# A LoRA layer folded into a mixture of low-rank experts: W dealt by strided rows, B turned on VectorE, G sent through DRAM

## The chip, the core and the metric

The kernel runs on one core of one Trainium2 chip, in one launch. The metric is the device time of that core in microseconds. All data are float32. The engines are TensorE (PE in the profile, with PEld for its weight loads), VectorE (DVE), ScalarE (ACT), GpSimd (POOL) and SyncE (SP); SyncE only issues DMAs here. All DMAs of the core share 16 DMA engines.

## The reference

```python
# x: 8 x 512 x 2048; W: 2048 x 2048; b: 2048
# lora_As: 32 x 2048 x 16; lora_Bs: 32 x 16 x 2048; one slot for each batch row
# route_w: 8 x 2048; A: 8 x 16 x 2048; Bw: 8 x 2048 x 16
A_b = lora_As[slot]; B_b = lora_Bs[slot]
y = einsum('bti,oi->bto', x, W) + b + 2.0 * einsum('btr,bro->bto', einsum('bti,bir->btr', x, A_b), B_b)
logits = einsum('bsd,ed->bse', y, route_w)
top_v, top_i = top_k(logits, 1)
weight = one_hot(top_i, 8) * top_v
h = einsum('bsd,erd->bser', y, A)
out = x + einsum('bser,eor->bso', weight[..., None] * h, Bw)
```

y itself is never needed, only its products with 136 columns: the 8 x 16 rows of A and the 8 rows of route_w, which the kernel calls proj (2048 x 136).

## The kernel before

**What it computes.** In a first stage the kernel forms C = W^T proj (2048 x 136), the bias row c0 = b proj, and G = 2 B proj, where B holds the 16 rows of each of the eight batch rows' slots, 128 rows in all. The matrix of batch row b is M_b = C + A_b G_b. The second stage multiplies each of the 32 token tiles of x (128 tokens x 2048) by its M_b (`heads`, ph), adds c0 and routes on VectorE (`route`), turns the routed 128 columns (`turn_heads`, pw), multiplies by ffn_b (`delta`, po) and adds the result to x (`add_delta`).

**The first stage.** W comes in 16 tiles of 128 rows (`load_w`, four buffers, SyncE's queue). For each, `chunk_w` copies the two halves of the tile's columns into an order of its own, the first on ScalarE and the second on VectorE (wv, two buffers each), and then the next free W buffer is loaded. `fold_w` multiplies the 16 chunks of a tile by that tile's rows of proj (pj), into six banks of PSUM (pc) that sum over the 16 tiles. A float32 matmul counts as two passes, so a W tile is 32 passes.

**Around it.** The order of every engine's work is written by hand: each engine takes its instructions in the order of the program, under a manual schedule, and a loop over oc (the W tiles) places everything else between the W products:
- `load_adapters_b` (after tile 4) works out the row numbers of B on VectorE and GpSimd gathers them from memory (raw, first half); `load_adapters_a` (after tile 7) does the same for A. The bias is loaded on GpSimd's queue.
- `turn_adapters` (tiles 8 to 10) transposes B in 16 TensorE transposes into pbT, and ScalarE copies them to ad_bT.
- `fold_bias` (tiles 9 and 10) sums bias times proj on VectorE, 16 instructions, into bp.
- `project_bias` and `project_adapters` (after tile 11) are the matmuls pb and pg; VectorE takes G to g_sb.
- `spread_g` (after tile 12 and within tile 13) brings the 32 rows of G of each pair of batch rows to all four quadrants of 32 partitions, by four matmuls with `eyes`, four stacked identities, into pq; VectorE multiplies each by a half mask into g4.
- `first_products` are the products A_0 G_0 (pa) from quadrants of 32 rows; they stand after tile 13, within 14 and after 14. After tile 15 VectorE adds them to C (m) and ScalarE keeps C (c).
- `spread_a` and `shuffle` copy A and x into quadrants, on GpSimd and ScalarE; `turn_x` transposes x on VectorE in blocks of 32 x 32 into xT.

Lines of before that the text names: L132 warm matmuls, L101 W loads, L95 proj loads, L274 W copies, L285 W products (pc), L316 and L317 B transposes and their copies, L307 and L309 bias products, L323 pb, L330 pg, L333 g_sb, L339 pq, L348 g4, L361 pa, L452 ph.

**DMA queues.** Plain loads and stores are issued by SyncE (q1 in the profile) and ScalarE (q10), gathers by GpSimd (q0). Eight semaphores take turns over the DMAs of SyncE and ScalarE, so a DMA waits for the earlier one on its semaphore. SyncE issues in order; after W come ffn_b (fb) and x_1 and x_2, in two tiles of 1 MB each.

Of the kernel before, what the change touches and what calls it, by code (L numbers as in the profile page):

```python
# [9 lines left out]
F32 = mybir.dt.float32  # L10
# [8 lines left out]
def kernel(  # L19
# [27 lines left out]

    nc = tc.nc  # L50
    P = 128
    Q = 32
# [21 lines left out]
    qpool = ctx.enter_context(tc.tile_pool(name="qpool", bufs=2))  # L74
    tpool = ctx.enter_context(tc.tile_pool(name="tpool", bufs=3))
    small = ctx.enter_context(tc.tile_pool(name="small", bufs=2))
    wctx = ctx.enter_context(ExitStack())
    wpool = wctx.enter_context(tc.tile_pool(name="wpool", bufs=1))
    ps_s = ctx.enter_context(tc.tile_pool(name="ps_s", bufs=2, space=bass.MemoryType.PSUM))
# [9 lines left out]

    it_i = const.tile([P, B], I32, name="it_i")  # L90
    pj = wpool.tile([P, NO, NP], F32, name="pj")
    proj_v = proj.rearrange("(c p) e -> p c e", p=P)

    def load_pj(c0, c1, eng=nc.sync):
        eng.dma_start(out=pj[:, c0:c1, :], in_=proj_v[:, c0:c1, :])  # L95
# [2 lines left out]

    def load_w(oc):
        wt = wpool.tile([P, D], F32, tag="w", bufs=4, name=f"w_{oc}")  # L100
        nc.sync.dma_start(out=wt, in_=w[ts(oc, P), :])  # L101
        w_tiles.append(wt)

    load_pj(0, 1, nc.scalar)
    load_w(0)
    load_w(1)
    load_pj(3, 5)
    load_w(2)
    load_pj(5, 8)
    load_w(3)  # L110

    x_tiles = {}
# [12 lines left out]
    make_identity(nc, ident)  # L125

    nc.scalar.copy(warm_a[:, 1:2], warm_a[:, :1])
    load_pj(1, 3, nc.scalar)
    nc.scalar.dma_start(out=it_i, in_=itok.to_broadcast([P, B]))
    pm = ps_s.tile([P, P], F32, tag="s", name="pm")  # L130
    for _ in range(14):
        nc.tensor.matmul(pm, warm, warm, start=True, stop=True)  # L132

    own_i = const.tile([P, B], I32, name="own_i")
# [11 lines left out]
    rank = const.tile([P, E], F32, name="rank")  # L146
    nc.vector.tensor_copy(rank, rank_i)

    raw = qpool.tile([P, 2, D], F32, tag="q", name="raw")
    ad_b = raw[:, 0, :]  # L150
    ad_ar = raw[:, 1, :]
    fb = const.tile([P, D], F32, name="fb")
    bias_o = const.tile([P, NO], F32, name="bias_o")

    brow_f = const.tile([P, 1], F32, name="brow_f")

    def load_adapters_b():

        it_f = const.tile([P, B], F32, name="it_f")
        nc.vector.tensor_scalar(it_f, it_i, float(R), None, ALU.mult)  # L160
        row_f = const.tile([P, B], F32, name="row_f")
        nc.vector.tensor_tensor(row_f, it_f, own, ALU.add)
        nc.vector.tensor_tensor(row_f, row_f, mask, ALU.mult)
        nc.vector.tensor_reduce(brow_f, row_f, AX.X, ALU.add)
        brow_i = const.tile([P, 1], I32, name="brow_i")
        nc.vector.tensor_copy(brow_i, brow_f)  # L166
        nc.gpsimd.indirect_dma_start(  # L167
            out=ad_b,
            out_offset=None,
            in_=cond_b,  # L170
            in_offset=bass.IndirectOffsetOnAxis(ap=brow_i, axis=0),
        )
        nc.gpsimd.dma_start(out=bias_o, in_=bias)

    def load_adapters_a():

# [8 lines left out]


    half = const.tile([P, 2], F32, name="half")

    def fill_constants():
        nc.vector.tensor_reduce(  # L190
            half, mask.rearrange("p (k h) -> p h k", h=2), AX.X, ALU.add
        )

# [8 lines left out]
    def spread_a(q, k, copy):  # L204
# [3 lines left out]
        if q < 2:  # L208
            copy(dst[:, 3:], src[:, ds(JC + 2 * q, 2)])

    ad_bT = tpool.tile([P, NJ, P], F32, tag="t", name="ad_bT")

    g4 = const.tile([P, B, NP], F32, name="g4")
# [4 lines left out]
    def turn(dst, src, h):  # L218
# [2 lines left out]
            dst[:, ts(h, HJ), :].rearrange("p j (g t) -> p g j t", t=Q),  # L221
            src.rearrange("p g (j a) -> p g j a", a=Q)[:, :, ts(h, HJ), :],
        )


    eyes = const.tile([P, NQ, Q], F32, name="eyes")
    nc.vector.tensor_reduce(
        eyes[:, 0, :], ident.rearrange("p (q c) -> p c q", c=Q), AX.X, ALU.add
    )
    nc.vector.tensor_copy(eyes[:, 1:, :], eyes[:, :1, :].to_broadcast([P, NQ - 1, Q]))  # L230

    xq_tiles = {}
    moves = [(g, i) for i in range(NQ) for g in range(NQ)]
# [26 lines left out]
    def chunk_w(oc):  # L260
        copies = (nc.scalar.copy, nc.vector.tensor_copy)
        wv = [
            wpool.tile([P, HJ, P], F32, tag=f"wv{h}", bufs=2, name=f"wv{h}_{oc}")
            for h in range(2)
        ]
        wr = w_tiles[oc].rearrange("p (i j a) -> p j i a", i=NQ, a=Q)
        for h in range(2):
            wv_tiles[oc, h] = wv[h]
            dst = wv[h].rearrange("p j (i a) -> p j i a", a=Q)

            n = HJ // 2 if oc == 0 else HJ
            for k in range(HJ // n):
                copy = copies[1 - k] if oc == 0 else copies[h]
                copy(dst[:, ts(k, n)], wr[:, ds(h * HJ + k * n, n)])  # L274
        if oc + 4 < NO:
            if oc in (0, 1):
                load_pj(8 + 4 * oc, 12 + 4 * oc)
            load_w(oc + 4)

    def fold_w(oc, within=None):  # L280
        for q, (pc, (j0, n)) in enumerate(zip(pcs, groups)):
            for k in range(n):

                h, j = divmod(j0 + k, HJ)
                nc.tensor.matmul(  # L285
                    pc[:, k, :],
                    wv_tiles[oc, h][:, j, :],
                    pj[:, oc, :],
                    start=(oc == 0 and k == 0),
                    stop=(oc == NO - 1),  # L290
                    skip_group_check=True,
                )
            if oc == NO - 1:
                k, jk = divmod(j0, JC)
                c, m = (part[k][:, ds(jk, n), :] for part in (cs, ms[0]))
                nc.vector.tensor_tensor(m, m, pc[:, :n, :], ALU.add)
                nc.scalar.copy(c, pc[:, :n, :])
            if q == 2 and within:
                within()


    bp = wpool.tile([P, NP], F32, name="bp")

    def fold_bias(js):
        for j in js:
            if j == 0:
                nc.vector.tensor_scalar(bp, pj[:, 0, :], bias_o[:, :1], None, ALU.mult)  # L307
            else:
                nc.vector.scalar_tensor_tensor(  # L309
                    bp, pj[:, j, :], bias_o[:, j : j + 1], bp, ALU.mult, ALU.add  # L310
                )

    def turn_adapters(g):
        pt = ps_s.tile([P, 4, P], F32, tag="s", name=f"pbT_{g}")
        for k in range(4):
            nc.tensor.transpose(pt[:, k, :], ad_b[:, ts(4 * g + k, P)], ident)  # L316
        nc.scalar.copy(ad_bT[:, ts(g, 4), :], pt)  # L317

    g_sb = wpool.tile([P, NP], F32, name="g_sb")

    def project_bias():
        pb = ps_s.tile([P, NP], F32, tag="s", name="pb")
# [9 lines left out]
            )  # L332
        nc.vector.tensor_scalar(g_sb, pg, COND_SCALING, None, ALU.mult)  # L333

    def spread_g(ks):

        for k in ks:
            pq = ps_s.tile([P, NP], F32, tag="s", name=f"pq_{k}")
            nc.tensor.matmul(  # L339
                pq,  # L340
                eyes[ts(k, Q)].rearrange("p q c -> p (q c)"),
                g_sb[ts(k, Q), :],
                start=True,
                stop=True,
                tile_position=(k * Q, 0),
            )
            for h in range(2):
                nc.vector.tensor_scalar(  # L348
                    g4[:, 2 * k + h, :], pq, half[:, h : h + 1], None, ALU.mult
                )  # L350


    pieces = [(0, 3 * q, 3, q) for q in range(NQ)] + [(1, 2 * q, 2, q) for q in range(2)]
# [17 lines left out]
        part, j0, nj, _ = pieces[z]  # L371
        return (t[part][:, ds(j0, nj), :] for t in (ms[b % 2], cs))

    def first_products(some, copy=nc.vector.tensor_copy):
        banks = {
            z: ps_s.tile([P, GRP, NP], F32, tag="s", name=f"pa_{z}") for z in some
        }
        adapter_products(0, some, banks)
        for z in some:
            m, _ = place(0, z)  # L380
            copy(m, banks[z][:, : pieces[z][2], :])

    chunk_w(0)
    for oc in range(NO):
        if oc + 1 < NO:
            chunk_w(oc + 1)
        fold_w(
            oc,
            {
                13: lambda: spread_g((2, 3)),  # L390
                14: lambda: first_products((2, 3)),
            }.get(oc),
        )
        if oc == 2:
            fill_constants()
        if oc == 4:
            load_adapters_b()
        if oc == 7:
            load_adapters_a()
        for g in {8: (0,), 9: (1, 2), 10: (3,)}.get(oc, ()):  # L400
            turn_adapters(g)
        if oc in (9, 10):
            fold_bias(range(8 * (oc - 9), 8 * (oc - 8)))
        if oc == 8:
            load_x(0)
            for k in range(NQ):
                for q in range(3):
                    spread_a(q, k, nc.gpsimd.tensor_copy)
            shuffle(0, moves[6:], nc.gpsimd.tensor_copy)
        if oc == 11:  # L410
            for k in range(NQ):
                spread_a(3, k, nc.scalar.copy)
            nc.sync.dma_start(out=fb, in_=ffn_b)
            load_x(1)
            load_x(2)
            project_bias()
            project_adapters()
        if oc in (12, 13, 14):
            shuffle(0, moves[2 * (oc - 12) : 2 * (oc - 11)], nc.scalar.copy)
        if oc == 12:  # L420
            spread_g((0, 1))
        if oc == 13:
            first_products((0, 1))
        if oc == 14:
            first_products((4, 5), nc.scalar.copy)
            for h in range(2):
                turn_x(0, h)
    wctx.close()
# [254 lines left out]
```

## Time and profile before

| | before |
|---|---|
| median of 3 runs | 326.51 us (326.3 to 326.63) |
| profiled execution | 326.17 us, span 324.4 us |
| TensorE busy | 318.7 us (98%), granted clock 1.0 |
| VectorE, ScalarE, GpSimd busy | 230.1, 185.4, 164.9 us |
| DMA | 88.52 MB, mean 273 GB/s |
| first stage ends (first ph) | 76.86 us |

The times come from one profiled execution. The page gives the busy time of each engine, the span in 40 slices (each digit is the busy share in tenths), the DMA queues, and the chain of work that ended last. The timeline lists instructions in order of time: start, length, engine, line, operation, output and inputs, count, and in brackets the idle time before and what ended it. Matmuls overlap, so a row's length reaches past the start of the next one; lengths of steps on TensorE are taken from start to start.

### The profile page before, as it was taken

Reading aid. Unit: us, or ns where it says so; the run is one execution under the profiler, and the core shown is the slowest. Engines: PE = TensorE matmul, PEld = TensorE weight load, DVE = VectorE, ACT = ScalarE, POOL = GpSimd, SP = SyncE. Lnnn points to the kernel's source line nnn. Section 1 sums busy time; section 2 is a strip of 40 time slices with the busy share of each in tenths; the row PEclk is TensorE's granted clock in tenths of the full one; section 3 lists DMA queues with packets and bytes.
Section 4 is the critical chain, followed back from the end, with each engine's and each line's share of the span. In section 5 each row is a group of like instructions: output and inputs, shape, how many; then the busy total and the mean of one; then the engine's idle time right before and its main releaser. Section 6 shows DMA issues by size and latency. Waiting matters only on the chain.

```text
span 324.4 us, 5611 instructions
## 1 busy us (share of the span) xinstructions
PE 318.7 (98%) x2168; PEld 252.6 (78%) x2168; DVE 230.1 (71%) x408; ACT 185.4 (57%) x230; POOL 164.9 (51%) x180
## 2 busy tenths in 40 slices
PE   8999999999999999999999999999999999999994
PEld 8999999999776777777768677767676777766762
DVE  2123183468879788887887888788787887888864
ACT  3223247527958567748764976596567758770000
POOL 1002149998967676257717771946295357710000
PEclk9999999999999999999999999999999999999999
DMA  7999999953933385859395949585876759334437
GB/s 281 365 404 421 420 418 420 421 231 120 401 129 129 131 284 235 301 233 368 153 375 229 361 165 395 184 353 165 355 255 266 270 250 358 162 162 179 174 144 250
DMA packets 15306, 88.52 MB, mean 273 GB/s; under 512 B 1696, under 2 KB 4016, under 8 KB 4912
## 3 DMA queue, kind: packets, MB, share of 16 engines
q1 hardware_dynamic: 14112, 85.45, 67.2%
q0 software_dynamic: 320, 2.11, 1.6%
q10 hardware_dynamic: 848, 0.61, 0.6%
q8 instruction: 17, 0.28, 0.4%
q14 instruction: 9, 0.07, 0.1%
HBM read 54.60 MB, written 33.55 MB: 272 GB/s over the span
## 4 chain that ended last, share of the span: by engine, by line
PE 94%; DMA 4%; SPq 0%; ACT 0%; DVE 0%; issue 0%; DVEq 0%; ACTq 0%
PE ph L452 37%; PE po L546 32%; PE pc L285 16%; PE pa L361 4%; DMA w<-in_w_dram 4%; PE pg L330 1%; PE pw L508 1%; PE pe_o L546 1%; PE pbT L316 1%; PE pe_h L546 1%; ACT wv L274 0%; DVE x L559 0%; PE pq L339 0%; PE pe_s L546 0%; SPq L101 0%; SPq L95 0%
## 5 line engine op out<-in xcount | busy, mean ns | idle before, releaser
L242 POOL COPY xq<-x 32x1024 f32<-32x1024 f32 x121 | 126.7, 1047 | 77.4 <-DMA x<-in_x_dram 26.7
L242 ACT COPY xq<-x 32x1024 f32<-32x1024 f32 x135 | 140.9, 1044 | 12.0 <-DMA x<-in_x_dram 10.0
L452 PEld LDWEIGHTS ph<-m,xT 128*128 128x128 f32 x1024 | 124.7, 190 | 20.6 <-issue 16.1
L452 PE MATMUL ph<-m,xT 128*128 128x136 f32 x1024 | 129.5, 280 | 0.0
L546 PE MATMUL po<-fb,whT 128*128 128x512 f32 x240 | 111.6, 592 | 0.0
L559 DVE TENSOR_TENSOR x<-x,po 128x1024 f32<-128x1024 f32 x60 | 72.9, 1216 | 30.6 <-PE po L546 30.4
L220 DVE STREAM_TRANSPOSE xT<-xq 128x1024 f32<-128x1024 f32 x64 | 78.9, 1236 | 2.4 <-ACT xq L242 2.4
L546 PEld LDWEIGHTS po<-fb,whT 128*128 128x128 f32 x240 | 41.7, 190 | 32.0 <-issue 32.0
L285 PE MATMUL pc<-pj,wv 128*128 128x136 f32 x512 | 61.7, 280 | 0.2 <-ACT wv L274 0.2
L285 PEld LDWEIGHTS pc<-pj,wv 128*128 128x128 f32 x512 | 60.1, 190 | 1.1 <-ACT wv L274 0.4
L513 ACT COPY whT<-pw 128x128 f32<-128x128 f32 x32 | 8.5, 267 | 54.8 <-PE pw L508 54.5
L274 DVE COPY wv<-w 128x1024 f32<-128x1024 f32 (+1 forms) x17 | 12.7, 754 | 30.8 <-PE pc L285 17.8
L274 ACT COPY wv<-w 128x1024 f32<-128x1024 f32 (+1 forms) x17 | 16.9, 998 | 28.5 <-DMA w<-in_w_dram 21.8
L504 POOL TENSOR_TENSOR m<-m,c 128x408 f32<-128x408 f32 (+1 forms) x28 | 24.5, 905 | 1.3 <-ACT m L499 0.8
L499 ACT COPY m<-pa 128x408 f32<-128x408 f32 (+1 forms) x28 | 10.4, 456 | 17.6 <-PE pa L361 17.6
L167 POOL DMA_INDIRECT raw<-in_cond_b_dram,brow_i x1 | 1.4, 1434 | 24.4 <-DVE brow_i L166 24.4
L361 PE MATMUL pa<-g,ad_q 32*128 32x136 f32 x256 | 12.7, 288 | 0.0
L361 PEld LDWEIGHTS pa<-g,ad_q 32*128 32x128 f32 x256 | 10.6, 184 | 1.3
L207 POOL COPY ad_q<-raw 32x384 f32<-32x384 f32 x12 | 6.4, 536 | 9.3 <-DMA raw<-in_cond_a_dram,arow_i 8.9
L508 PEld LDWEIGHTS pw<-ident,wh 128*128 128x128 f32 x32 | 4.5, 141 | 7.4 <-issue 7.2
L463 DVE TENSOR_TENSOR ph<-ph,c0b 128x136 f32<-128x136 f32 x32 | 9.1, 284 | 1.5 <-PE ph L452 1.5
L473 DVE TENSOR_TENSOR wh<-ph,rw 128x128 f32<-128x128 f32 x32 | 9.3, 291 | 1.1
(65 smaller groups left out, 119.7 us busy)
## 6 DMA issues: line engine op xcount, KB each, us to landing
x<-in_x_dram SPq DMA_DIRECT2D x32, 1024.0 KB, 9.3
out_dram<-x SPq DMA_DIRECT2D x30, 1024.0 KB, 4.9
w<-in_w_dram SPq DMA_DIRECT2D x16, 1024.0 KB, 11.4
out_dram<-x SPq DMA_DIRECT2D x6, 256.0 KB, 2.7
fb<-in_ffn_b_dram SPq DMA_DIRECT2D x1, 1024.0 KB, 13.7
pj<-in_proj_dram SPq DMA_DIRECT2D x2, 272.0 KB, 10.8
out_dram<-x ACTq DMA_DIRECT2D x1, 256.0 KB, 2.4
pj<-in_proj_dram SPq DMA_DIRECT2D x1, 204.0 KB, 11.3
```

Source lines behind the costliest of these rows:

```text
L220: nc.vector.transpose(dst[:, ts(h, HJ), :].rearrange("p j (g t) -> p g j t", t=Q), src.rearrange("p g (j a) -> p g j a", a=Q)[:, :, ts(h, ...
L242: copy(xq_tiles[u][ts(i, Q), :, g, :], x_tiles[u][ts(g, Q), :, ts(i, DQ)])
L274: copy(dst[:, ts(k, n)], wr[:, ds(h * HJ + k * n, n)])
L285: nc.tensor.matmul(pc[:, k, :], wv_tiles[oc, h][:, j, :], pj[:, oc, :], start=(oc == 0 and k == 0), stop=(oc == NO - 1), skip_group_check= ...
L361: nc.tensor.matmul(banks[z][:, n, :], ad_q[ts(q, Q), b // 2, 3 * part + n, :], g4[ts(q, Q), b, :], start=True, stop=True, tile_position=(q ...
L452: nc.tensor.matmul(ph_tiles[t][:, :NP], xT_tiles[t][:, j, :], m[j // JC][:, j % JC, :], start=(j == 0), stop=(j == NJ - 1),)
L463: nc.vector.tensor_tensor(ph, ph, c0b, ALU.add)
L473: nc.vector.tensor_tensor(wh.rearrange("p (e r) -> p e r", r=R), ph[:, :ER].rearrange("p (e r) -> p e r", r=R), rw.unsqueeze(2).to_broadca ...
L499: nc.scalar.copy(m, pa)
L504: nc.gpsimd.tensor_tensor(m, m, c, ALU.add)
L546: nc.tensor.matmul(part, whT_tiles[t], fb[:, ds(c, n)], start=True, stop=True)
L559: nc.vector.tensor_tensor(xs, xs, part, ALU.add)
```

## The change

W is dealt by rows 16p + c instead of 128c + p: tile c holds, on partition p, row 16p + c of W, and pj holds the rows of proj in the same order, so that each partition's rows of proj are contiguous in memory. C is a sum over all rows and does not depend on the order; the bias and the columns of B must follow it.
- Tile 0 is loaded in two DMAs, each with half of the columns; proj comes in four loads (columns 0, 1-2, 3-7, 8-15) instead of six. Three warm matmuls are left out.
- The bias is loaded on ScalarE's queue at the start, in the old order. In `fill_constants` VectorE builds two sums of the identity and the product bias_m, one TensorE matmul (pb_o) puts the bias in order, VectorE copies it. `fold_bias` moves to tiles 6 and 7.
- B is turned without TensorE: `spread_b` copies 16 blocks of 32 x 512 into quadrants (bq; 4 on ScalarE, 12 on VectorE, tiles 8 and 9) and `turn_b` transposes them on VectorE, two halves (tiles 10 and 11).
- G goes to the quadrants through memory: after tile 12's copies are issued ScalarE writes g_sb to DRAM (g_dram), reads it back in four DMAs (gq, `spread_g`), and VectorE multiplies by the half mask in two instructions (`halve_g`, after tile 13). The three groups of `first_products` move by half a tile: within 14, after 14, within 15, and all their copies are on ScalarE. After tile 15 the copies of C wait for two groups.
- In the program load_x(2) stands after project_adapters.

On the engines: ScalarE issues the write of G behind its W copy for tile 13, then shuffles two blocks of x, then issues the four reads, then copies W tile 14. VectorE's products `halve_g` stand between its W copies for tiles 14 and 15. By the DMAs' semaphores x_1's second tile is issued when W tile 15 has landed, x_2's first when ffn_b has landed, and its second when the write of G has landed; before, their waits were for W tiles 12 and 13 and x_0.

```diff
-    proj_v = proj.rearrange("(c p) e -> p c e", p=P)
+    proj_v = proj.rearrange("(p c) e -> p c e", p=P)
+    w_v = w.rearrange("(p c) d -> c p d", p=P)
...
-        nc.sync.dma_start(out=wt, in_=w[ts(oc, P), :])
+
+        n = HJ if oc == 0 else NJ
+        for k in range(NJ // n):
+            dst, src = (
+                m.rearrange("p (i c) -> p i c", i=NQ)[:, :, ds(k * n * Q, n * Q)]
+                if oc == 0
+                else m
+                for m in (wt, w_v[oc])
+            )
+            nc.sync.dma_start(out=dst, in_=src)
         w_tiles.append(wt)
...
-    load_pj(3, 5)
+    load_pj(1, 3)
     load_w(2)
-    load_pj(5, 8)
+    load_pj(3, 8)
...
-    load_pj(1, 3, nc.scalar)
     nc.scalar.dma_start(out=it_i, in_=itok.to_broadcast([P, B]))
     pm = ps_s.tile([P, P], F32, tag="s", name="pm")
-    for _ in range(14):
+    for _ in range(11):
...
-    raw = qpool.tile([P, 2, D], F32, tag="q", name="raw")
-    ad_b = raw[:, 0, :]
-    ad_ar = raw[:, 1, :]
+    ad_b = tpool.tile([P, NJ, P], F32, tag="t", name="ad_b").rearrange("p j a -> p (j a)")
+    ad_ar = qpool.tile([P, 2, D], F32, tag="q", name="ad_ar")[:, 0, :]
     fb = const.tile([P, D], F32, name="fb")
+    bias_n = const.tile([P, NO], F32, name="bias_n")
+    nc.scalar.dma_start(out=bias_n, in_=bias)
...
-        nc.gpsimd.dma_start(out=bias_o, in_=bias)
...
     def fill_constants():
         nc.vector.tensor_reduce(
             half, mask.rearrange("p (k h) -> p h k", h=2), AX.X, ALU.add
         )
+
+        nm = P // NO
+        by_c = wpool.tile([P, NO], F32, name="by_c")
+        nc.vector.tensor_reduce(
+            by_c, ident.rearrange("p (m c) -> p c m", c=NO), AX.X, ALU.add
+        )
+        by_m = wpool.tile([P, nm], F32, name="by_m")
+        nc.vector.tensor_reduce(
+            by_m, ident.rearrange("p (m c) -> p m c", c=NO), AX.X, ALU.add
+        )
+        nc.vector.tensor_tensor(
+            bias_m,
+            bias_n.unsqueeze(2).to_broadcast([P, NO, nm]),
+            by_m.unsqueeze(1).to_broadcast([P, NO, nm]),
+            ALU.mult,
+        )
+        pb = ps_s.tile([P, NO], F32, tag="s", name="pb_o")
+        nc.tensor.matmul(
+            pb, bias_m.rearrange("p k m -> p (k m)"), by_c, start=True, stop=True
+        )
+        nc.vector.tensor_copy(bias_o, pb)
...
+    bq = tpool.tile([P, NQ, DQ], F32, tag="t", name="bq")
     ad_bT = tpool.tile([P, NJ, P], F32, tag="t", name="ad_bT")
...
-    eyes = const.tile([P, NQ, Q], F32, name="eyes")
-    nc.vector.tensor_reduce(
-        eyes[:, 0, :], ident.rearrange("p (q c) -> p c q", c=Q), AX.X, ALU.add
-    )
-    nc.vector.tensor_copy(eyes[:, 1:, :], eyes[:, :1, :].to_broadcast([P, NQ - 1, Q]))
...
-            if oc in (0, 1):
-                load_pj(8 + 4 * oc, 12 + 4 * oc)
+            if oc == 0:
+                load_pj(8, 16)
             load_w(oc + 4)
 
     def fold_w(oc, within=None):
+        kept = []
...
                 k, jk = divmod(j0, JC)
                 c, m = (part[k][:, ds(jk, n), :] for part in (cs, ms[0]))
                 nc.vector.tensor_tensor(m, m, pc[:, :n, :], ALU.add)
-                nc.scalar.copy(c, pc[:, :n, :])
+                kept.append((c, pc[:, :n, :]))
             if q == 2 and within:
                 within()
+            if q >= 2:
+                for c, m in kept:
+                    nc.scalar.copy(c, m)
+                kept.clear()
...
-    def turn_adapters(g):
-        pt = ps_s.tile([P, 4, P], F32, tag="s", name=f"pbT_{g}")
-        for k in range(4):
-            nc.tensor.transpose(pt[:, k, :], ad_b[:, ts(4 * g + k, P)], ident)
-        nc.scalar.copy(ad_bT[:, ts(g, 4), :], pt)
+    def spread_b(ms, copy):
+        for g, i in ms:
+            copy(bq[ts(i, Q), g, :], ad_b[ts(g, Q), ts(i, DQ)])
+
+    def turn_b(h):
+        nc.vector.transpose(
+            ad_bT[:, ts(h, HJ), :].rearrange("p c (g t) -> p g c t", t=Q),
+            bq.rearrange("p g (a c) -> p g c a", c=NO)[:, :, ts(h, HJ), :],
+        )
 
     g_sb = wpool.tile([P, NP], F32, name="g_sb")
+    g_dram = dram.tile([P, NP], F32, name="g_dram")
+    gq = wpool.tile([P, NQ, NP], F32, name="gq")
...
-    def spread_g(ks):
-
-        for k in ks:
-            pq = ps_s.tile([P, NP], F32, tag="s", name=f"pq_{k}")
-            nc.tensor.matmul(
-                pq,
-                eyes[ts(k, Q)].rearrange("p q c -> p (q c)"),
-                g_sb[ts(k, Q), :],
-                start=True,
-                stop=True,
-                tile_position=(k * Q, 0),
+    def spread_g():
+
+        for q in range(NQ):
+            nc.scalar.dma_start(
+                out=gq[ts(q, Q)], in_=g_dram.rearrange("(k s) e -> s k e", s=Q)
             )
-            for h in range(2):
-                nc.vector.tensor_scalar(
-                    g4[:, 2 * k + h, :], pq, half[:, h : h + 1], None, ALU.mult
-                )
+
+    def halve_g():
+
+        for h in range(2):
+            nc.vector.tensor_scalar(
+                g4.rearrange("p (k h) e -> p h k e", h=2)[:, h],
+                gq,
+                half[:, h : h + 1],
+                None,
+                ALU.mult,
+            )
...
-            copy(m, banks[z][:, : pieces[z][2], :])
...
+        if oc == 12:
+            nc.scalar.dma_start(out=g_dram, in_=g_sb)
         fold_w(
             oc,
             {
-                13: lambda: spread_g((2, 3)),
-                14: lambda: first_products((2, 3)),
+                14: lambda: first_products((0, 1)),
+                15: lambda: first_products((4, 5)),
             }.get(oc),
...
+        if oc in (6, 7):
+            fold_bias(range(8 * (oc - 6), 8 * (oc - 5)))
         if oc == 7:
             load_adapters_a()
-        for g in {8: (0,), 9: (1, 2), 10: (3,)}.get(oc, ()):
-            turn_adapters(g)
-        if oc in (9, 10):
-            fold_bias(range(8 * (oc - 9), 8 * (oc - 8)))
...
             shuffle(0, moves[6:], nc.gpsimd.tensor_copy)
+        if oc in (8, 9):
+            ms_b = moves[oc % 2 :: 2]
+            spread_b(ms_b[:2], nc.scalar.copy)
+            spread_b(ms_b[2:], nc.vector.tensor_copy)
+        if oc in (10, 11):
+            turn_b(oc - 10)
         if oc == 11:
             for k in range(NQ):
                 spread_a(3, k, nc.scalar.copy)
             nc.sync.dma_start(out=fb, in_=ffn_b)
             load_x(1)
-            load_x(2)
             project_bias()
             project_adapters()
+            load_x(2)
         if oc in (12, 13, 14):
             shuffle(0, moves[2 * (oc - 12) : 2 * (oc - 11)], nc.scalar.copy)
         if oc == 12:
-            spread_g((0, 1))
+            spread_g()
         if oc == 13:
-            first_products((0, 1))
+            halve_g()
         if oc == 14:
-            first_products((4, 5), nc.scalar.copy)
+            first_products((2, 3))
             for h in range(2):
                 turn_x(0, h)
```

More of the change, by code (lines that the diff above doesn't have):

```diff
@@ L76 @@
     small = ctx.enter_context(tc.tile_pool(name="small", bufs=2))
+    dram = ctx.enter_context(tc.tile_pool(name="dram", bufs=1, space=bass.MemoryType.DRAM))
     wctx = ctx.enter_context(ExitStack())
@@ L187 @@
     half = const.tile([P, 2], F32, name="half")
+    bias_m = wpool.tile([P, NO, P // NO], F32, name="bias_m")
     def fill_constants():
@@ L372, in place, with first_products @@
         return (t[part][:, ds(j0, nj), :] for t in (ms[b % 2], cs))
-    def first_products(some, copy=nc.vector.tensor_copy):
+    def first_products(some):
         banks = {
@@ L380, in first_products @@
             m, _ = place(0, z)
-            copy(m, banks[z][:, : pieces[z][2], :])
+            nc.scalar.copy(m, banks[z][:, : pieces[z][2], :])
     chunk_w(0)
```

## The prediction

> **What bounds the kernel now.** I read the page first: engine totals, slices, chain.
>
> ```profile
> PE 318.7 (98%) x2168; PEld 252.6 (78%) x2168; DVE 230.1 (71%) x408; ACT 185.4 (57%) x230; POOL 164.9 (51%) x180
> DMA  7999999953933385859395949585876759334437
> PE 94%; DMA 4%; SPq 0%; ACT 0%; DVE 0%; issue 0%; DVEq 0%; ACTq 0%
> ```
>
> TensorE is busy 98% of the span and is 94% of the chain. A step taken off it shortens the kernel by its own length, and a wait put on it lengthens it. The second line says what else is scarce, but only early: the DMA engines are full through the whole of the first stage.
>
> Next the timeline of TensorE in that stage; the first number is the start, the second the length.
>
> ```profile
> 1.06 6.16 PE L132 MATMUL pm<-warm 128*128 128x128 f32 x28 [1.06 <-DVE warm_a L87]
> 14.87 26.21 PE L285 MATMUL pc<-pj,wv 128*128 128x136 f32 x224 [0.23 <-ACT wv L274]
> 40.92 0.60 PE L316 MATMUL pbT<-ident,raw 128*128 128x128 f32 x4
> 41.36 3.87 PE L285 MATMUL pc<-pj,wv 128*128 128x136 f32 x32
> ...
> 57.73 3.87 PE L285 MATMUL pc<-pj,wv 128*128 128x136 f32 x32
> 61.53 0.50 PE L339 MATMUL pq<-g_sb,eyes 32*128 32x136 f32 x4
> 61.96 2.35 PE L285 MATMUL pc<-pj,wv 128*128 128x136 f32 x18
> 64.25 0.50 PE L339 MATMUL pq<-g_sb,eyes 32*128 32x136 f32 x4
> 64.68 1.89 PE L285 MATMUL pc<-pj,wv 128*128 128x136 f32 x14
> 66.50 0.96 PE L361 MATMUL pa<-g,ad_q 32*128 32x136 f32 x12
> ...
> 76.86 6.65 PE L452 MATMUL ph<-m,xT 128*128 128x136 f32 x56
> ```
>
> Start to start, 32 passes of a W tile take 3.72 us (26.05/224 a pass, 14.87 to 40.92). The only idle time is 0.4 us before 14.87, behind the third W tile. The second stage starts at 76.86 and is TensorE alone to the end, so the question is when that row starts afterwards.
>
> Last the DMA queues, q1 (SyncE's) and q10 (ScalarE's), in stretches: packets, MB, share of the engines. Two for 2.5 to 6 us, then q1 alone for 66 to 67 and for 68 to 69. Below them are two landings from the page.
>
> ```profile
> q1 hardware_dynamic: 168, 1.25, 86.2%
> q10 hardware_dynamic: 164, 0.08, 8.4%
> q1 hardware_dynamic: 60, 0.41, 98.6%
> q1 hardware_dynamic: 48, 0.33, 79.0%
> ```
> ```profile
> pj<-in_proj_dram ACTq DMA_DIRECT2D x1, 136.0 KB, 7.9
> it_i<-in_itok_dram ACTq DMA_DIRECT2D x1, 4.0 KB, 9.6
> ```
>
> From 2.5 to 6 us both queues have work, and each sends as many packets as the other, 168 against 164, though q1's are 8 KB and q10's 544 bytes or less. Such a pair takes 16 x 3.5/164 = 0.34 us on an engine. So a small load on ScalarE's queue moves at the pace of the large packets: 512 little rows (128 and 256 of proj, 128 of itok), issued from 0.74, had landed only at 1.68 + 9.6 = 11.3. And q1 stays full until 68: that is W, then ffn_b and four x tiles.
>
> **Part by part.** *B on VectorE instead of TensorE.* The 16 transposes go: 0.44 (40.92 to 41.36), 0.87 and 0.44, together 1.75 us off the path. The 16 quarter copies (12 VectorE, 4 ScalarE) and two stream transposes lie beside the W products: six copies at 0.4 (the 128x512 copy) and a W copy of 0.7 to 0.8 are 3.2 of a 3.72 us tile, and the last transpose (1.24) ends near 51, before pg needs it at 52.4. Cost nothing; uncovered, 1.2.
>
> *Masked bias.* VectorE gets two reductions (0.37, the eyes row), a product (about 0.3) and a copy after its fourth W copy, which ended at 17.7; the product is ready near 18.8 and TensorE comes by at 18.59. One small matmul plus that wait: between 0.23 (the pb row) and 0.6; I take 0.5. The two blocks of bias products (8 x 0.37 each) move from tiles 9, 10 to 6, 7 and stand ahead of arow_i on VectorE: the A gather leaves at 37.8 instead of 34.7. GpSimd's spreads and shuffles behind it then end at 69.6 instead of 66.6; VectorE turns x_0 by 72.1, which is covered as long as the second stage starts after 73.
>
> *Head.* Three warm matmuls fewer (six passes of 0.21, 1.3 us), W tile 0 in two halves of 1 KB rows, proj in rows of 1 to 4 KB instead of 544 bytes. Tile 0's first half can be used near 5.8, but tiles 1 and 2 decide: they come behind 1024 packets of 1 KB, at 0.05 each (between 544 bytes at 0.035 and the 1.2 KB mean of the last stores at 0.059) 3.2 us per engine where eight of 0.29 took 2.3; fewer little rows give back 0.5 to 1.5. So from 0.6 lost to 1.3 won; I take 0.4 won.
>
> W's rows now lie 128 KiB apart in memory; no transfer of this trace has such a pitch, so a loss there can't be excluded from the rows (second rival). The Trainium skill, "DMA: Bandwidth & Descriptors", section "Latency and other measured facts", has copies falling from 207 GB/s at a pitch of 512 KiB to 103 at 4 MiB, with about 214 as the full rate; no run here shows it, and read downwards it would make 128 KiB cost nothing.
>
> *G.* The four pq matmuls go: 4.23 - 3.72 = 0.51 for the first pair and 4.54 - 3.72 - 0.19 (the switch into pa, which stays) = 0.63 for the second, 1.14 in all. In their place: g_sb, a write to DRAM, four reads, two products on VectorE, and only then pa(0,1), in the middle of tile 14. pg ends at 57.73 - 1.75 + 0.5 - 0.4 = 56.1, g_sb at 56.6. From there TensorE needs 3.72 x 2 + 2.3 us and would reach pa(0,1) at 65.9.
>
> The write has 128 rows of 544 bytes, like the first proj load on the same queue, which was issued at 0.74 and had landed by 6.2, when SyncE's wait for it ended: 5.5 us. The other end is the store on that queue late in the kernel, 2.4. q1 is as full as at the start, so 5.5: landed at 62.1. Only then does ScalarE issue the reads, 4 x 0.4 us. Its W copy for tile 14 stands behind them and ends at 64.8, where TensorE wants it at 63.6; a stall that vanishes in the next one.
>
> The reads are 512 rows, 32 per engine and four semaphore packets. The first moves near 63.4. q1 ran dry about 69.2 before; with some 1.7 us less of small proj rows, 0.8 more for tile 0 and 0.3 for G's write, now near 68.6. That leaves 5.2/0.29 = 18 large packets per engine: 18 pairs of 0.34 take until 69.5, the rest 18 x 0.03 until 70. The last x tile, issued about 51.9, landed 19.8 later at 71.7, some 2 after its queue ran dry; the same lag puts G at 71.8. Ends: 63.6 (a write in 2.4, reads in 1.6 + 3.0, the short store) and 72.6 (62.1 + the 10.5 of the 512 rows at the start).
>
> The page of the skill named above says, in "Queues, rings and completion order", that an engine drains a packet of some 9 to 17 descriptors from one ring before it turns to the next. By that, G's nine per engine would go in one turn and the reads in four, landing near 66. The 168 against 164 say otherwise, and I go by them.
>
> Products of 544 columns lie between 0.35 (136 columns) and 0.8 (the copy of 1024): two at 0.45, so pa(0,1) starts at 72.8 and TensorE has waited 6.9 us. Behind the waiting instruction on VectorE stand its W copy for tile 15 and the turning of x_0, neither late again. From pa(0,1) to the second stage it is 0.89 + 1.82 + 0.90 + 2.28 + 0.66 + 1.75 = 8.3, so 81.1 against 76.86: +4.2.
>
> Then the clock after the pause. The granted clock reads 1.0 even at the start, yet there TensorE, coming from rest, took 0.21 us a pass for 28 passes and 0.116 later: 2.6 us lost. No row shows a pause in mid-kernel, so 0 to 2.6. The start is the nearest row, the pause is shorter: I take 1.8.
>
> Sum against the profiled execution, 326.17 (span 324.4): +4.2 + 1.8 = 332.2. The median of the runs shown lies 0.3 higher; I leave it at 332.2.
>
> **Rivals.** *G in time (faster).* If q1 is dry or yields, all 1.75 + 1.14 + 0.4 - 0.5 = 2.8 us are won: 323.4. It decides at a landing of 64.8 for no stall, and the change breaks even with 67.6 (76.86 - 8.3 - 1.0). For it: x_1's second tile and x_2 now wait for earlier landings before they are issued, so q1's backlog is shorter. Against: w_15, ffn_b and x_1's first tile keep it fed until each next one is issued; I find no gap.
>
> *W's pitch (slower still).* The last W tile landed near 59 and is needed near 69, so W may lose 10 us over 16 tiles of 2.5 us, a quarter of its rate, before TensorE waits at the end; at half rate the last tile comes 40 us late and the kernel takes some 354. A loss of a quarter shows first at tiles 2 to 4, 1 to 2 us each. Nothing in the profile speaks for it.
>
> *G late by a little.* Landing about 67.6: 326.
>
> **How the numbers follow.** Late G 0.72, by itself 328 to 336 (landing 70 to 72.6 with the clock's 0 to 2.6, head and lag loose by 1). G in time 0.16, slightly late 0.04, pitch 0.08. About 0.2%, 0.65 us, is what a measurement can tell from no change. Faster 0.18, same 0.03, slower 0.79. The range reaches down to the faster case, 323.3, and leaves out the pitch and the edges.
>
> **What would show it.** Right: no idle TensorE until tile 14, then 5 to 7 us before the first pa row with VectorE's g product as releaser and that waiting on DMA gq; q10 and q1 with equal packets from 63 to 68; ph from 81 to 83. Wrong: gq landing before 66; W copies waiting on DMA after tile 4; an A spread or x_0's turn as the last to be ready; pbT's cover gone, with pg waiting for ad_bT.

## The result, and the profile after

The changed kernel takes 335.04 us (median of 6 runs, 332.89 to 337.65) against 326.44 before (6 runs): a ratio of 1.0265, 95% interval 1.0222 to 1.0309. It is slower, as forecast, and 2.8 us above the 332.2 of the prediction, inside its range. The profiled execution took 337.65 us (span 335.9). It is the slowest of the six, and its mean granted clock, 0.978, the lowest (0.983 to 0.989 in the others, 1.000 before), so the lines below overstate the median's loss of 8.6 us by some 3.

The page of the changed kernel, the lines shown before (engines, granted clock in tenths, chain):

```profile
PE 322.1 (96%) x2140; PEld 255.6 (76%) x2140; DVE 235.9 (70%) x414; ACT 187.2 (56%) x234; POOL 163.0 (49%) x179
PEclk9999999975999999999999999999999999999999
PE 89%; DMA 7%; DVE 1%; ACTq 0%; ACT 0%; SPq 0%; issue 0%; DVEq 0%
```

DMA has 7% of the chain instead of 4, and two of the forty slices have a clock well below full. The timeline of TensorE in the first stage, then, from the whole timeline, ScalarE's and VectorE's part, and from the chain of waits the two DMAs of G:

```profile
12.20 7.68 PE L313 MATMUL pc<-pj,wv 128*128 128x136 f32 x64 [1.03 <-ACT wv L301]
...
57.23 7.58 PE L313 MATMUL pc<-pj,wv 128*128 128x136 f32 x64
67.52 3.78 PE L313 MATMUL pc<-pj,wv 128*128 128x136 f32 x18 [2.71 <-ACT wv L301]
75.11 1.73 PE L400 MATMUL pa<-g,ad_q 32*128 32x136 f32 x12 [3.81 <-DVE g L383]
76.77 3.54 PE L313 MATMUL pc<-pj,wv 128*128 128x136 f32 x14
...
88.22 3.98 PE L497 MATMUL ph<-m,xT 128*128 128x136 f32 x33
```
```profile
64.39 1.94 ACTq L376 DMA_DIRECT2D gq<-g_dram  x4
66.42 1.04 ACT L301 COPY wv<-w 128x1024 f32<-128x1024 f32 x1 [6.12 <-issue]
74.11 2.04 DVE L383 TENSOR_SCALAR g<-gq,half 128x544 f32<-128x544 f32 x2 [12.19 <-DMA gq<-g_dram]
```
```profile
57.77 6.60 DMA g_dram<-g_sb
65.86 8.12 DMA gq<-g_dram
```

The second stage starts at 88.22 instead of 76.86, 11.4 us later, and the profiled executions differ by 11.5: all of the loss lies ahead of that row. G leaves at 57.77, is in memory at 64.39 and back at 74.0. Meanwhile TensorE has two pauses: the first W product of tile 14 waits for ScalarE's W copy, which stands behind the reads, and pa(0,1) waits for VectorE's product of the reads. The third part of the loss shows in the stretches of time; the last three numbers of a row are the granted clock, the DMA share and GB/s:

```profile
71.30:75.10 3.80, 0.00 (x1) 0.02 (x1) 0.99 (x2) 0.00 (x0) 3.62 (x5) 0.95 0.14 36
75.10:80.20 5.10, 5.09 (x26) 4.64 (x26) 2.73 (x3) 2.99 (x4) 4.93 (x5) 0.50 0.00 0
80.20:83.00 2.80, 2.80 (x18) 2.51 (x18) 2.14 (x2) 0.90 (x2) 2.68 (x4) 0.50 0.00 0
83.00:85.80 2.80, 2.80 (x15) 2.70 (x14) 1.16 (x2) 0.00 (x0) 0.87 (x1) 0.59 0.00 0
85.80:88.20 2.40, 2.40 (x23) 2.23 (x23) 1.16 (x2) 1.60 (x5) 0.00 (x0) 1.00 0.04 7
```

After the pause TensorE works at half the clock, by the 0.59 of the fourth row until about 85.3, and waits for nobody: from pa(0,1) to ph it is 13.1 us instead of 8.3.

### The profile page after: what moved, and what is told of

It is laid out like the page before. It is cut to its first block, busy times and chain, and to the rows that moved or that the text cites. A ratio compares the mean times of both kernels' runs of the same rounds, so it can differ in the third digit from the quotient of the medians.

```text
span 335.9 us, 5566 instructions
## 1 busy us (share of the span) xinstructions
PE 322.1 (96%) x2140; PEld 255.6 (76%) x2140; DVE 235.9 (70%) x414; ACT 187.2 (56%) x234; POOL 163.0 (49%) x179
## 4 chain that ended last, share of the span: by engine, by line
PE 89%; DMA 7%; DVE 1%; ACTq 0%; ACT 0%; SPq 0%; issue 0%; DVEq 0%
PE ph L497 36%; PE po L591 31%; PE pc L313 15%; PE pa L400 4%; DMA w<-in_w_dram 3%; DMA gq<-g_dram 2%; DMA g_dram<-g_sb 2%; PE pg L368 1%; PE pw L553 1%; PE pe_o L591 1%; PE pe_h L591 1%; ACTq L376 0%; ACT wv L301 0%; DVE x L604 0%; SPq L113 0%; DVE g L383 0%
## 5 line engine op out<-in xcount | busy, mean ns | idle before, releaser
L313 PE MATMUL pc<-pj,wv 128*128 128x136 f32 x512 | 66.6, 294 | 4.4 <-ACT wv L301 3.7
L313 PEld LDWEIGHTS pc<-pj,wv 128*128 128x128 f32 x512 | 65.0, 203 | 5.6 <-ACT wv L301 4.1
L400 PE MATMUL pa<-g,ad_q 32*128 32x136 f32 x256 | 14.2, 303 | 3.8 <-DVE g L383 3.8
L400 PEld LDWEIGHTS pa<-g,ad_q 32*128 32x128 f32 x256 | 12.0, 197 | 5.4 <-issue 4.3
L179 POOL DMA_INDIRECT ad_b<-in_cond_b_dram,brow_i x1 | 1.1, 1128 | 24.5 <-DVE brow_i L178 24.5
L240 POOL COPY ad_q<-ad_ar 32x384 f32<-32x384 f32 x12 | 6.0, 499 | 10.9 <-DMA ad_ar<-in_cond_a_dram,arow_i 10.4
L383 DVE TENSOR_SCALAR g<-gq,half 128x544 f32<-128x544 f32 x2 | 2.0, 1062 | 12.2 <-DMA gq<-g_dram 12.2
## 6 DMA issues: line engine op xcount, KB each, us to landing
w<-in_w_dram SPq DMA_DIRECT2D x15, 1024.0 KB, 11.5
```

What stands on the lines that cost most here:

```text
L313: nc.tensor.matmul(pc[:, k, :], wv_tiles[oc, h][:, j, :], pj[:, oc, :], start=(oc == 0 and k == 0), stop=(oc == NO - 1), skip_group_check= ...
L400: nc.tensor.matmul(banks[z][:, n, :], ad_q[ts(q, Q), b // 2, 3 * part + n, :], g4[ts(q, Q), b, :], start=True, stop=True, tile_position=(q ...
```

## The experiments

**G by matmuls, the rest of the change kept.** The old `spread_g` in its old places; the pa products in the new ones.

```diff
-            nc.scalar.dma_start(out=g_dram, in_=g_sb)          # and the four reads, halve_g
+            spread_g((0, 1))                                   # after tile 12; (2, 3) within tile 13
```

> The changed kernel with G brought to the quadrants by the four matmuls of before (tile 12 and within tile 13) instead of through DRAM; W by strided rows, the two halves of tile 0, the masked bias and B on VectorE stay, and so do the new places of the pa products. Theory (all of the loss is G's way through DRAM and the clock that falls behind it): pg still ends near 57.2, no pause in tile 14, clock 1.0 throughout, first ph at 57.2 + 19.1 = 76.4 against 76.86 before, so 326.0, within 0.5. Rival (the dealing of W, the turning of B on VectorE or the later gather of A costs on its own): slower than 327, with a wait on DMA w, ad_bT or xq ahead of ph.

325.57 us (11 runs) against 326.3 on the same chips, ratio 0.9977 (0.9968 to 0.9986). TensorE in this run:

```profile
8.80 2.12 PE L318 MATMUL pc<-pj,wv 128*128 128x136 f32 x16 [0.82 <-DVE wv L306]
11.97 7.68 PE L318 MATMUL pc<-pj,wv 128*128 128x136 f32 x64 [1.05 <-ACT wv L306]
57.01 3.87 PE L318 MATMUL pc<-pj,wv 128*128 128x136 f32 x32
76.13 6.65 PE L496 MATMUL ph<-m,xT 128*128 128x136 f32 x56
```

No pause, clock 1.0, ph at 76.13. So all of the loss is G's way through memory, and the rest of the change gains 0.7 us. The two idle times at the start are new, a point for the last run but two.

**G through DRAM alone, in the kernel before.** Everything else as before, but the pa products and load_x(2) in their new places.

```diff
-            spread_g((0, 1))
+            nc.scalar.dma_start(out=g_dram, in_=g_sb)          # reads and halve_g as in the change
```

> The kernel of before with one part of the change alone: G through DRAM on ScalarE's queue, with the new places of the pa products and of load_x(2). Theory: the same pause as in the changed kernel, g_dram landing 6 to 7 us after its issue near 58.4, the reads 9 to 10 us later near 74.5, half clock after the pause, 333 to 338 in all. Rival (the pause needs the other parts, for instance ScalarE's copies of B or the emptier queue): under 330.

335.42 us, ratio 1.030 (1.0265 to 1.0335). The write took 6.6 us from its issue at 58.53, pa(0,1) started at 75.11, ph at 85.73. This one part makes the whole loss; it needs none of the others, and its new places alone cost nothing in the run before. The two pauses and ph:

```profile
68.26 2.35 PE L281 MATMUL pc<-pj,wv 128*128 128x136 f32 x18 [2.69 <-ACT wv L269]
75.11 1.73 PE L364 MATMUL pa<-g,ad_q 32*128 32x136 f32 x12 [4.50 <-DVE g L347]
85.73 6.53 PE L457 MATMUL ph<-m,xT 128*128 128x136 f32 x55
```

The first pause is as long as the changed kernel's (2.69 us against 2.71), but no half clock follows it: the granted clock is 1.00 from 66 to 70. It is 0.50 from 75 to 80, behind the second pause, and from pa(0,1) to ph it is 10.6 us. This profiled execution took 335.06 us at a mean clock of 0.989, close to the changed kernel's median. So what the clock costs a usual run of it is, as an estimate, rather the 2.3 us of this run (10.6 - 8.3) than the 4.8 of its own profiled execution.

**Wider rows.** G in memory so that each partition reads one row of 2176 bytes: 12 packets per engine for the reads instead of 36.

```diff
-                out=gq[ts(q, Q)], in_=g_dram.rearrange("(k s) e -> s k e", s=Q)
+                out=gq[ts(q, Q)].rearrange("s k e -> s (k e)"), in_=g_dram
...
-            nc.scalar.dma_start(out=g_dram, in_=g_sb)
+            for k in range(NQ):
+                nc.scalar.dma_start(out=g_dram[:, ts(k, NP)], in_=g_sb[ts(k, Q), :])
```

> The changed kernel with G stored in DRAM so that each partition reads one row of 2176 bytes instead of four of 544: reads of 3 packets per engine and DMA instead of 9, 12 instead of 36 in all; the write becomes four DMAs of 32 rows (12 packets per engine instead of 9). Theory (ScalarE's queue gets one packet for each of SyncE's, whatever the size): write landed near 65 to 66, reads 12 pairs of 0.34 later or when q1 is dry, near 72 instead of 74.0; total 2 us below the changed kernel, within 1.5. Rival (an engine drains nine or more descriptors of one queue at a turn, so their number doesn't matter): reads land 8 to 10 us after their issue as before, total the same or worse by the three more issues.

337.17 us (ratio 1.0343), no faster: the reads landed 6.9 to 9.4 us after their issue, with a third of the packets. Neither side is confirmed by it, since the three further DMAs also moved SyncE's waits: the last x tile was issued at 65, just ahead of the reads, and landed 10.9 later, so the queue that the reads had to share ran dry at 75 instead of 71. From 72 to 73 q10 sent 33 packets beside 34 of q1: one for one again, at 0.48 us a pair (16 engines, 33 pairs in a microsecond) instead of 0.34. The first packet of the reads moved only 3.5 us after their issue. That silence was a hint that my account of the delay lacked something.

**G ahead of x_1 and x_2.** The write and the reads on SyncE's queue behind ffn_b, x_1 and x_2 behind them.

```diff
-            load_x(1)                                          # ahead of project_bias
+            nc.sync.dma_start(out=g_dram, in_=g_sb)            # after tile 12
+            spread_g()                                         # four reads, on nc.sync
+            load_x(1)
+            load_x(2)
```

> The changed kernel with G's write and reads issued by SyncE, behind ffn_b and ahead of x_1 and x_2, so that no large transfer is queued beside the reads. Theory (the backlog of x tiles is what delays G): write lands near 62, when ffn_b is through, reads near 65.5, pa(0,1) at 67.0 with no pause of over 1 us and no half clock; ScalarE no longer stands behind the reads; first ph near 75.5, total 324.8 to 326. x_1 then lands near 70, which costs nothing if GpSimd's shuffles of x_0 (until 72) are later anyway. Rival (reading DRAM just written is slow by itself): reads still land 8 us after issue, pause of 3 us or more, over 329.

325.9 us (11 runs), ratio 0.999 (0.9981 to 1.0). The landing of the reads, then TensorE:

```profile
DMA to landing us min/median/max: 1.8/2.1/2.4
```
```profile
57.20 9.66 PE L313 MATMUL pc<-pj,wv 128*128 128x136 f32 x82
66.79 0.96 PE L400 MATMUL pa<-g,ad_q 32*128 32x136 f32 x12
75.13 6.73 PE L496 MATMUL ph<-m,xT 128*128 128x136 f32 x56
83.28 1.98 PE L590 MATMUL po<-fb,whT 128*128 128x512 f32 x4 [0.39 <-ACT whT L557]
85.68 2.12 PE L496 MATMUL ph<-m,xT 128*128 128x136 f32 x16 [0.42 <-DVE xT L254]
```

The same reads take 2 us instead of 8, and TensorE never pauses in the first stage after the start. ph begins 1.7 us earlier than before, a little more than worked out; 1.3 of it is given back in the second stage (from ph to the row at 85.68 it is 10.55 us, to the same row before, at 86.10, it was 9.24). There TensorE waits for copies of x. GpSimd stood still for x_1 only 0.45 us, until 72.56, so how much of the 1.3 is the late x_1 is open; my "costs nothing" does not hold for the stage.

**x_2 behind the reads.** G on ScalarE's queue as in the change, but x_2 is issued only when the reads are.

```diff
+            nc.scalar.copy(xt[:, :, :1], fill2)                # on x_2, behind the four reads
             nc.sync.dma_start(out=xt[:, k, :], ...)            # so the load waits for it
```

> The changed kernel, G through DRAM on ScalarE's queue as there, but x_2 is issued only after ScalarE has issued the reads (ScalarE writes one column of the x_2 tile first, which the load replaces). Everything ahead of the reads stays: ffn_b, both tiles of x_1. In the changed kernel the first packet of the reads moved 3.6 us after their issue, at the time when the last x tile issued ahead of them began to move. Theory (a small DMA starts only when the large ones issued before it on the other queue have all begun, and shares packet for packet from then on): write lands near 64.4 as before, reads start within 1.5 us and land by 68 to 70 instead of 74; total 330 to 333. Rival (packets are shared from the start and nothing else delays them, as the prediction had it): x_2 now runs beside all 36 packets per engine, reads land near 77, total above 337.

331.12 us, ratio 1.0136 (1.011 to 1.0161): 3.9 below the changed kernel. The write landed at 64.3 as before, the reads 2.1 to 3.1 us after their issue. Queues q1 and q10 from 65 to 66, then q10 from 67 to 68, where q1 has no packet at all:

```profile
q1 hardware_dynamic: 20, 0.11, 27.4%
q10 hardware_dynamic: 112, 0.05, 24.2%
q10 hardware_dynamic: 278, 0.13, 52.7%
```

With x_1's last tile nearly through, the first packet of the reads moves 1.0 us after their issue (3.3 in the changed kernel), and they soon have the engines to themselves. The first pause (ScalarE's W copy behind the reads) is still 3.4 us and the half clock follows it: from pa(0,1) at 72.53 to ph at 83.11 it is 10.6 us.

**Warm matmuls in the pauses.**

```diff
+            fill(12)                                           # between tiles 13 and 14
...
-                14: lambda: first_products((0, 1)),
+                14: lambda: (fill(24), first_products((0, 1))),
```

> The changed kernel with warm matmuls in TensorE's two pauses: 12 between tiles 13 and 14 (about 2.6 us) and 24 within tile 14 ahead of pa(0,1) (about 5.1 us); nothing waits for them. Theory (the pause itself lets the clock fall to one half, and that costs 4 to 5 us after it): G lands as before near 74, clock 1.0 throughout, pa(0,1) to the first ph in 8.4 us instead of 13.1, total 329.5 to 332. Rival (the clock falls for another reason, or the slow stretch is the wait of copies): no faster than the changed kernel, 334 or more.

333.5 us (ratio 1.0233), its profiled execution 333.45. TensorE, and the clock from 74 to 84 us:

```profile
69.78 5.52 PE L425 MATMUL pf<-warm 128*128 128x128 f32 x48
75.23 1.15 PE L400 MATMUL pa<-g,ad_q 32*128 32x136 f32 x12
83.69 6.53 PE L503 MATMUL ph<-m,xT 128*128 128x136 f32 x55
```
```profile
74.00:84.00 10.00, 10.00 (x93) 9.22 (x92) 7.75 (x10) 5.83 (x12) 9.46 (x9) 1.00 0.01 2
```

G is as late as before (pa at 75.23 against 75.11), the clock stays at 1.0, and from pa(0,1) to ph it is 8.5 us instead of 13.1. So the pause itself lets the clock fall. The two profiled executions differ by 4.2 us, the medians only by 1.5. That the changed kernel's other runs lost less to the clock than the profiled one fits their mean clocks (0.983 to 0.989 against 0.978) and the 2.3 us of the run with G through DRAM alone, but they left no trace that would show it. My range for this run was built on the profiled one and was 1.5 too low.

**Tile 0 of W in one load**, on the run with G by matmuls.

```diff
-        n = HJ if oc == 0 else NJ
+        n = NJ
```

> The run with G by matmuls (325.6), and W tile 0 in one load of 8 KB rows again instead of two halves of 1 KB rows. Theory (the 1024 packets of 1 KB hold back tile 0's second half and tile 1): tile 0 lands near 6.0 and tile 1 near 8.7 as in the kernel before, no wait in tile 0 and none ahead of tile 1, tile 2 starts near 14.7 to 15 instead of 15.8; total 324.4 to 324.9, below both kernels. Rival (the strided rows or the proj rows hold back the start): tile 2 starts no earlier, total 325.4 or more.

324.44 us, ratio 0.9945 (0.9931 to 0.9959): below both kernels.

```profile
6.23 3.97 PE L318 MATMUL pc<-pj,wv 128*128 128x136 f32 x32 [0.18 <-DVE wv L306]
10.86 7.65 PE L318 MATMUL pc<-pj,wv 128*128 128x136 f32 x64 [0.66 <-ACT wv L306]
55.94 3.87 PE L318 MATMUL pc<-pj,wv 128*128 128x136 f32 x32
75.07 6.65 PE L496 MATMUL ph<-m,xT 128*128 128x136 f32 x56
```

The wait inside tile 0 is gone and everything after it is 1.1 us earlier. Tile 1 landed at 9.7, not at 8.7 as I expected, so 0.66 of idle time stays; why it is later than before was not tried.

**A probe.** In that version one more small load, which nothing waits for, while W is streaming: 128 rows of 544 bytes on ScalarE's queue.

```diff
+        if oc == 3:
+            nc.scalar.dma_start(out=probe, in_=proj_v[:, 0, :])
```

> The run with G by matmuls and tile 0 in one load, and beside it one DMA that nothing waits for: 128 rows of 544 bytes of proj to a tile of their own, issued by ScalarE behind its copy of W tile 4, near 22, when SyncE's queue is full and holds some 8 to 10 us of W tiles issued before. Theory (a small DMA starts to move only when the large ones issued before it have begun): its first packet moves 5 us or more after the issue, near the start of the W tile issued last before it. Rival (it starts at once and shares packet for packet): first packet within 1.5 us, the last within 5 us of the issue.

One execution, 324.27. The probe was issued at 21.21 and landed 6.9 us later. q1 from 23 to 24, then q1 and q10 from 24 to 25 and from 26 to 27:

```profile
q1 hardware_dynamic: 60, 0.41, 98.7%
q1 hardware_dynamic: 56, 0.41, 98.3%
q10 hardware_dynamic: 12, 0.01, 2.3%
q1 hardware_dynamic: 59, 0.38, 91.6%
q10 hardware_dynamic: 61, 0.03, 11.4%
```

No packet of it moved before 24, and the first near 24.7, 3.5 us after the issue; then the queues shared packet for packet. The W tile issued last before it (17.49, landed 28.8) comes behind the ones that landed at 23.7 and 26.2, so by its place in the queue it began near 24; that is an estimate, no row shows its first packet. The rival's 1.5 us is out, and the 5 us of my own expectation was too long. The order fits my theory, but this run does not tell it from a start that is some 3 us late whenever q1 is full. Against a fixed delay speaks that the reads' first packet came 2.1 us after the issue with G through DRAM alone and with warm matmuls, and 3.3 and 3.5 in the changed kernel and with wider rows.

**G ahead of x_1 and x_2, tile 0 in one load.**

> G through DRAM on SyncE's queue ahead of x_1 and x_2 (325.9 before), with W tile 0 in one load. If the first stage's end alone counted, 1.1 us less: 324.8. GpSimd's shuffle of x_0 ended at 72.1 there and x_1 landed after 72, which both bind before TensorE does, so I expect 325 to 325.7, not below the run with matmuls and tile 0 whole (324.44). Rival (the route through DRAM is the better one once it is not delayed): below 324.4.

324.82 us (12 runs), ratio 0.9967 (0.9949 to 0.9986), 0.2 under my range. ph starts at 74.44, ahead of the version with matmuls (75.07), and the total is no better; the intervals of the two overlap. Through DRAM or by matmuls makes no clear difference once G isn't delayed.

## Why the prediction was right, and where its sizes were off

The forecast, slower by G's way through DRAM and by the clock, was right in its mechanism, and the two runs that take that part out or put it in alone show it. Several of its signs did not come as given: TensorE stood idle for 1.7 us at the head (0.67 and 1.03), where it had none before tile 14; G landed at 74.0, past the 72.6 taken as the late end; equal packets came from 68 to 70, not from 63; ph was at 88.2, not 81 to 83; 2.7 us of the pause stood ahead of tile 14, so that 3.8 were left before pa. In the profiled execution the term furthest off is the clock's. By its steps, with the second stage at 88.2 instead of the forecast 82.9 (81.1 and 1.8 for the clock):

- **Head and bias: 1.1 us too early.** pg ended at 57.23, not 56.1. The head lost 1.0 (tile 2 at 15.9 instead of 14.87) where I took 0.4 as won, outside my range of 0.6 lost to 1.3 won. The price of a 1 KB packet was right: from 2 to 5 us, 754 packets of q1 took 78.3% of 16 engines for 3 us, 0.05 each. But from 5 to 8 us q1 used only 67%: the second half of tile 0 arrived at 8.6 with engines to spare, and that I had not allowed for. The bias cost 0.14, not 0.5, since the product was ready at 18.9 and TensorE came at 19.7.
- **The write: 1.1 late.** 6.6 us against the 5.5 of the first proj load. That load was issued before any W tile; this write had ffn_b and an x tile ahead of it, and its first packet moved only 3.1 us after the issue.
- **The reads: right in sum, wrong in make-up.** Issue to landing was 9.6 us for 9.7 forecast. I had 18 pairs of packets from 1.3 us after the issue, and then the rest quickly. In fact the queue was silent for 3.6 us but for two packets, shared for two, and sent the rest when q1 ran dry. Queues q1 and q10 of the changed kernel from 67 to 68, 68 to 69 and 70 to 71:

```profile
q1 hardware_dynamic: 49, 0.31, 98.9%
q10 hardware_dynamic: 2, 0.00, 0.3%
q1 hardware_dynamic: 50, 0.38, 90.8%
q10 hardware_dynamic: 48, 0.03, 8.5%
q1 hardware_dynamic: 32, 0.17, 52.5%
q10 hardware_dynamic: 226, 0.11, 41.6%
```

 The sharing, 48 against 50, is the equality that the prediction read at the start; the silence before it is where I had 1.3 us. The probe and the run with x_2 behind the reads fit a start behind the tiles issued earlier; no run shows that this is its cause. With the silence and without it the reads end when q1 is dry, so that their length came out right is partly luck.
- **The products of the reads:** 2.0 us for the two instead of 0.9, but pa(0,1) needs only the first (0.86) and started 1.1 after the landing, where 1.0 was forecast. The stall of ScalarE's W copy, ahead of tile 14, was 2.7 instead of 1.2; I had rightly let it vanish in the later wait, but not seen that it starts the clock's fall.
- **The clock: 1.8 taken, 4.8 in the profiled execution.** The ends of 0 to 2.6 came from the start, where TensorE kept its slow pace for 5.9 us. Here the clock was at 0.50 from 68.3 to 71.6 and again from 75.1 to 85.3; in between, with TensorE idle, it read 1.0. This term carried the profiled execution out of my middle. At the median it is smaller if the run with G through DRAM alone is a guide: 2.3, inside my range, and then the 2.8 us above the forecast are, as an estimate, 1.1 of head and bias, 1.1 of the write and 0.5 of the clock. What spreads the runs over 4.8 us stays open: apart from the profiled run, their times do not follow their mean clocks (334.43 us at 0.983, 332.89 and 335.51 at 0.988).

On the rules weighed: by the Trainium skill, "DMA: Bandwidth & Descriptors", "Queues, rings and completion order", an engine drains some 9 to 17 descriptors of one ring before it changes; 48 against 50 here, with packets of very different size, speaks against it again. Equal counts could also come from turns of nine against nine, but the start times of single packets in the trace go mostly one large, one small. The same page's fall with a large row pitch, in "Latency and other measured facts", does not reach down to 128 KiB: W streams at the old rate. GB/s in the 40 slices of the changed kernel:

```profile
GB/s 205 420 423 420 421 418 421 401 179 0 111 391 127 125 127 352 157 380 218 370 155 373 230 274 264 235 371 176 380 201 374 156 349 251 251 128 163 180 159 250
```

Some 420 from the second to the seventh slice; before it was 418 to 421 from the fourth to the eighth. So the pitch, the second rival, is out. The faster rival, G in time, is what the runs with G ahead of x_1 gave (325.9): a smaller gain than its 323.4, as the head loses 1.0 instead of winning 0.4 and the second stage gives back 1.3.

## What to carry to other kernels

In these runs a small DMA in the critical chain took its time from what was queued when it was issued, on either queue: look at the backlog at its issue, not at its size, and issue it ahead of bulk loads or not at all. Four matmuls that cost 1.1 us in all and stall nobody can be cheaper than a trip through memory that takes them off the busiest engine. A pause of a busy TensorE can be paid twice, by itself and by the slow clock behind it; price both.

## What the runs showed of the hardware

- While SyncE's queue was full, a DMA on ScalarE's queue sent its first packet 2.1 to 3.5 us after its issue (the reads 2.1 with G through DRAM alone, 3.3 in the changed kernel; the probe 3.5), and 1.0 with that queue nearly dry. With nothing large queued, the same reads took 2.1 us from issue to landing. A start behind the tiles issued earlier fits this and is not shown to be its cause.
- Once both queues sent, they sent one packet each: 8 KB against 544 bytes (50 and 48 from 68 to 69) and, with wider rows, against 2176 bytes (34 and 33 from 72 to 73).
- An idle time of 2.7 us (64.8 to 67.5) was followed by a granted clock of 0.50 within 0.8 us of resuming in the changed kernel; one of the same length with G through DRAM alone was not, and there the clock fell only with the second pause, of 4.5 us. So the length of a pause alone did not decide it.
- With TensorE busy throughout, the half clock lasted 10.2 us after the second pause in the changed kernel (75.1 to 85.3), and some 5 us with G through DRAM alone (75.1 to 80.0) and with wider rows (77.3 to 81.9). From rest at the start the slow pace lasted 4.8 (G by matmuls) to 5.9 us (before).
- Two halves of 1 KB rows delayed a W tile by more than their engines' time: from 5 to 8 us, before the second half landed at 8.6, the DMA engines were 30% idle.
